# Gated projection in twelve-bit parts: its weights fetched, summed and split at fixed places ahead, every engine there kept in the written order

## The chip, the cores and the metric

The kernel runs on one core of a Trainium2 chip. The metric is device time in microseconds (us) of one execution. A core has a TensorE (PE in the profile, with its weight loads as PEld), a VectorE (DVE), a ScalarE (ACT), a GpSimd (POOL), and SyncE (SP), which here issues nearly all DMA transfers. Each engine works through its own list of instructions in order and waits on semaphores for the others.

## The reference, cut to what matters

A graph network: layer norm and ReLU of x, a batch norm, one graph convolution, four layers of cross attention and a gated feed-forward part, a second graph convolution, and two residuals. The changed code computes the two lines with `geglu_w` below.

```python
N, D, BS, M, DC, H, DH, L, E = (1024, 512, 16, 256, 512, 8, 64, 4, 16384)
h = _gcn(h, src, dst, gcn_in_w, gcn_in_b, n)
for i in range(L):
    a = _attn(_ln(h, ln2_w[i], ln2_b[i]), cond, Wq[i], Wk[i], Wv[i], Wo[i])
    h = h + a
    u = _ln(h, ln3_w[i], ln3_b[i]) @ geglu_w[i] + geglu_b[i]      # 1024x512 @ 512x4096
    val, gate = jnp.split(u, 2, axis=-1)
    f = val * jax.nn.gelu(gate, approximate=False)                # 1024x2048
    h = h + f @ ffo_w[i] + ffo_b[i]                               # 1024x2048 @ 2048x512
h = _gcn(h, src, dst, gcn_out_w, gcn_out_b, n)
```

## The kernel before, in words

**Seven products for eight.** All the large matrix products use Strassen-Winograd's form: a 2x2 block product by seven block products (numbered 0 to 6) and sums of blocks before and after them. In the gated projection the two column halves of the left operand are the value half and the gate half of the weights, so one pass gives value and gate of both halves of the rows.

**The stage.** The feed-forward part of a layer goes in four column blocks r = 0 to 3 of 512 values, each in four chunks c = 0 to 3 of 128. Block r = 0 is computed in plain fp32 (`Quad`, `geglu`). Blocks r = 1 to 3, that is twelve chunks in each of four layers, 48 in all, are objects of the class `Chunk`, in which each fp32 operand of six of the seven products is split into two parts of twelve bits and multiplied in the faster fp32r format: high times high and low times low (`begin`, line 1143), the result scaled on ACT (`scale`, L1151) or on DVE (`scale_onto`, L1155), and then the product of the sums added (`end`, L1160). Product 2 stays in plain fp32 (L1195).

**What a chunk needs.** Its weights are loaded by four DMAs on SP (L1125) into a tall tile `gxa` of 128x1024 and a low tile `gxb` of 128x512. POOL makes four block sums in place (L1127 to L1130). Then `split_left` makes three parts of each tile: the high part on ACT (L1101), the low part on DVE (L1102), and their sum on POOL (L1103). The tall parts feed products 0, 5, 6 and 4, the low ones 1 and 3. The split right operands are made once for a layer (`begin_right`, `finish_right`).

**What a chunk does.** `steps` is a generator: products 0, 5, 6, 4, 1, 3 begin in that order, their ends follow as the scalings come back, DVE adds the running sums s1, u2, u3 (L1184, L1186), makes the gate's input g1 (L1190), ACT applies Gelu (L1168), product 2 is added to the bank of product 4 (L1195), and DVE forms the two outputs (L1199, L1201, L1207) in `fT`. The loop over (r, c) interleaves the steps of a chunk with the last steps of the chunk before it. `sums_of_f` (L1275 to L1279, all on DVE) then makes the block sums that the output projection needs. After chunk 0 of the next block r stands the output projection of the block r - 1, `ffn_out`, in two halves of rows; its sums are added into `hall` and `kept` (L1306, L1310, L1318). `out_weights` makes the block sums of its weights on POOL (L216 to L219).

**What sets the order.** The program is written as a dataflow. A planner with its own model of durations places each instruction on its engine: of the instructions that it holds ready it takes the one written first, so work written later can go ahead of work that is not ready. The order written by hand holds only where `tc.keep_in_program_order` is put around an instruction; in this stage those are the matmuls of the chunks and of the `ffn_out` calls inside the loop. Wide tiles come from a pool of 36 `slot`s (128x1024 fp32), narrow ones from a pool of 10 `t512` tiles (128x512); a tile's first writer waits until the tile that had its room has been read for the last time. There are eight PSUM banks.

**How far ahead.** Two chunks are built before the loop and one more in each turn, after the chunk's fourth step, so that a chunk's transfer, sums and splits are written two chunks ahead of its use, and are placed by the planner.

Of the kernel before, what the change touches and what calls it, by code (L numbers as in the profile page):

```python
# [17 lines left out]
P = 128  # L18
# [7 lines left out]
def gnn_kernel(  # L26
# [1071 lines left out]

    def split_left(x, h, l, s):

        nc.scalar.mul(h.bitcast(F32R), x, INWARD * TINY)  # L1101
        nc.vector.scalar_tensor_tensor(l.bitcast(F32R), h, -1.0 / TINY, x, OP.mult, OP.add)  # L1102
        nc.gpsimd.tensor_tensor(s.bitcast(F32R), h, l, OP.subtract)  # L1103

    class Chunk:


        def __init__(self, l, r, c):
            self.n, self.c = f"{l}_{r}_{c}", c
            self.cv = l * 2 * DFF // P + r * KC + c  # L1110
            tall = [slot(f"g{n}a_{self.n}") for n in "xhls"]
            low = [t512(f"g{n}b_{self.n}") for n in "xhls"]
            self.last = t512(f"g4_{self.n}")[:, :2 * P].rearrange("p (k c) -> p k c", k=2)
            tall, low = ([t.rearrange("p a b -> p (a b)") for t in tall], low)

            def blocks(t):
                return t.rearrange("p (b k c) -> p b k c", k=2, c=P)

            self.parts = [[blocks(t) for t in of] for of in (tall, low)]
            a, b = (of.pop(0) for of in self.parts)  # L1120
            for k, (to, n) in enumerate(((a, 2), (b, 1))):
                for j in range(2):
                    c0 = j * DFF + r * D + c * P
                    of = geglu_w[l][2 * k * P:2 * (k + 1) * P, c0:c0 + P]
                    nc.sync.dma_start(to[:, n * j], of.rearrange("(k p) f -> p k f", p=P))  # L1125
            t = nc.gpsimd
            t.tensor_tensor(a[:, 3], a[:, 2], b[:, 1], OP.add)  # L1127
            t.tensor_tensor(a[:, 2], a[:, 0], a[:, 2], OP.subtract)
            t.tensor_tensor(a[:, 1], a[:, 3], a[:, 0], OP.subtract)
            t.tensor_tensor(self.last, b[:, 0], a[:, 1], OP.subtract)  # L1130
            for of in tall, low:
                split_left(*of)
# [4 lines left out]

        def begin(self, i):

            to = self.banks[i] = bank(f"g{i}_{self.n}")  # L1140
            for which in range(2):
                for k in range(2):
                    tc.keep_in_program_order(nc.tensor.matmul(  # L1143
                        to, self.part(i, which).bitcast(F32R)[:, k, :],
                        self.rights[i][which].bitcast(F32R)[:, k, :],
                        start=which + k == 0, stop=which + k == 2, skip_group_check=True))
            return to

        def scale(self, i):
            to = self.begin(i)  # L1150
            nc.scalar.mul(to, to, 1.0 + TINY)  # L1151

        def scale_onto(self, i, term):
            to = self.begin(i)
            nc.vector.scalar_tensor_tensor(to, to, 1.0 + TINY, term, OP.mult, OP.add)  # L1155

        def end(self, i):
            to = self.banks[i]
            for k in range(2):
                tc.keep_in_program_order(nc.tensor.matmul(  # L1160
                    to, self.part(i, 2).bitcast(F32R)[:, k, :],
                    self.rights[i][2].bitcast(F32R)[:, k, :],
                    start=False, stop=k == 1, skip_group_check=True))
            return to

        def gate(self, to, of):
            cg = self.cv + DFF // P
            nc.scalar.activation(to, of, AF.Gelu, bias=gcols[:, cg:cg + 1])  # L1168

        def steps(self):  # L1170
# [3 lines left out]
            add = nc.vector.tensor_tensor  # L1174
            self.banks = {}
            self.scale(0)
            yield
# [8 lines left out]
            add(u3, self.end(6), u2, OP.add)  # L1186
# [3 lines left out]
            add(g1, d, u3, OP.add)  # L1190
            self.gate(g1, g1)
            self.scale_onto(3, u3)
            yield
            for k in range(2):
                tc.keep_in_program_order(nc.tensor.matmul(  # L1195
                    d, self.last[:, k, :], self.rights[2][:, k, :], start=False, stop=k == 1,
                    skip_group_check=True))
            v1 = acc_tile(f"gv1_{n}")
            nc.vector.scalar_tensor_tensor(v1, d, bias, u2, OP.add, OP.add)  # L1199
            f0, f1 = (self.fT[i][self.c // 2][:, self.c % 2, :] for i in range(2))  # L1200
            add(f1, v1, g1, OP.mult)  # L1201
            yield
# [4 lines left out]
            nc.vector.scalar_tensor_tensor(f0, a, bias, g0, OP.add, OP.mult)  # L1207
# [62 lines left out]
    def sums_of_f(fT, s, c):  # L1270
# [3 lines left out]
        if c < 2:  # L1274
            nc.vector.tensor_tensor(a21, a11, a21, OP.subtract)  # L1275
        else:
            nc.vector.tensor_tensor(s2, a22, a21, OP.subtract)
            nc.vector.tensor_tensor(s1, s2, a11, OP.add)
            sums_of_f.last = nc.vector.tensor_tensor(s4, a12, s2, OP.subtract)  # L1279
# [10 lines left out]
    def ffn_out(l, r, s, left, right, kept, each=lambda ins: ins):  # L1290
# [14 lines left out]
        def add(to, of):  # L1305
            nc.vector.tensor_tensor(to, halves_of(of), to, OP.add)  # L1306

        product(0, a, True)
        if r:
            nc.vector.tensor_tensor(u, a, u, OP.add)  # L1310
# [7 lines left out]
        nc.vector.tensor_tensor(u, b, u, OP.add)  # L1318
# [195 lines left out]
    for l in range(L):  # L1514
# [430 lines left out]
```

## Time and profile before

| | |
|---|---|
| median of 3 runs | 2507.64 us (2507.08 to 2513.2) |
| the profiled execution, its own time | 2509.75 us |
| its span, first to last instruction | 2508.0 us |
| PE busy | 2417.6 us, 96% of the span |
| DVE busy | 1702.0 us, 68% |
| POOL busy | 1031.7 us, 41% |
| ACT busy | 842.4 us, 34% |
| mean granted clock of TensorE | 0.990 |

An instruction row names the line, the engine, the operation, what it writes and reads, the shapes, the count, the busy time and the mean of one, and the idle time of the engine just before with what ended it. A row of waits says who waited, for whom, for how long in total, how often, and the longest. In a timeline the bracket behind a row is the engine's idle time before it. A row of the windows view gives, for a stretch of the span, each engine's busy time and, in the column PEclk, the clock that TensorE was granted (1.00 is full speed). Busy times of PE are of a pipeline: a matmul's bar is longer than the distance to the next.

### The profile page before, as it was taken

Reading aid. Unit: us, or ns where it says so; the run is one execution under the profiler, and the core shown is the slowest. Engines: PE = TensorE matmul, PEld = TensorE weight load, DVE = VectorE, ACT = ScalarE, POOL = GpSimd, SP = SyncE. Lnnn points to the kernel's source line nnn. Section 1 sums busy time; section 2 is a strip of 40 time slices with the busy share of each in tenths; the row PEclk is TensorE's granted clock in tenths of the full one; section 3 lists DMA queues with packets and bytes.
Section 4 is the critical chain, followed back from the end, with each engine's and each line's share of the span. In section 5 each row is a group of like instructions: output and inputs, shape, how many; then the busy total and the mean of one; then the engine's idle time right before and its main releaser. Section 6 shows DMA issues by size and latency. Waiting matters only on the chain. (4 is left out here: it accounts for less than half of the span.)

```text
span 2508.0 us, 35114 instructions
## 1 busy us (share of the span) xinstructions
PE 2417.6 (96%) x13032; PEld 1888.5 (75%) x13032; DVE 1702.0 (68%) x3248; ACT 842.4 (34%) x1784; POOL 1031.7 (41%) x1059
## 2 busy tenths in 40 slices
PE   8999999999999999989999999999999999999999
PEld 5778886667787887567787888467777888567687
DVE  9656567777676557876776556777685556786764
ACT  7323334333213334342313333433223333433320
POOL 0433444265553223275453224264464322445541
PEclk9999999999999999999999999999999999999999
DMA  5422220111312210111221221011131031011140
GB/s 176 131 75 95 97 85 18 42 51 35 121 34 78 96 64 18 39 37 42 68 97 68 77 77 34 7 53 50 43 131 68 14 122 51 1 51 42 42 143 35
DMA packets 118066, 163.56 MB, mean 65 GB/s; under 512 B 9256, under 2 KB 66928, under 8 KB 117888
## 3 DMA queue, kind: packets, MB, share of 16 engines
q1 hardware_dynamic: 115792, 155.81, 19.1%
q0 software_dynamic: 1376, 4.30, 0.5%
q8 instruction: 107, 1.75, 0.3%
q10 hardware_dynamic: 720, 1.11, 0.1%
q14 instruction: 71, 0.58, 0.1%
HBM read 138.12 MB, written 23.07 MB: 64 GB/s over the span
## 5 line engine op out<-in xcount | busy, mean ns | idle before, releaser
L1151 ACT ACTIVATE g<-g 128x512 f32<-128x512 f32 x192 | 110.7, 579 | 349.4 <-PE g L1143 349.4
L1103 POOL TENSOR_TENSOR gsa<-gha,gla 128x1024 fp32r<-128x1024 f32 x48 | 131.8, 2746 | 193.1 <-DVE gla L1102 193.1
L1160 PE MATMUL g<-gr,gsa 128*128 128x512 f32 x384 | 128.2, 416 | 40.2 <-ACT g L1151 40.2
L1127 POOL TENSOR_TENSOR gxa<-gxa,gxb 128x256 f32<-128x256 f32 x48 | 41.1, 856 | 294.4 <-DMA gxa<-in_L_gnn_geglu_w_dram 250.8
L799 ACT ACTIVATE pr<-sc,nmax 128x256 f32<-128x256 f32 x256 | 118.4, 473 | 91.6 <-DVE nmax L794 91.1
L1143 PE MATMUL g<-gr,gha 128*128 128x512 f32 x384 | 144.3, 458 | 0.0
L300 PE MATMUL fa<-wff,fT 128*128 128x256 f32 x512 | 122.7, 383 | 5.0 <-DVE kept L1310 5.0
L1143 PE MATMUL g<-gl,gla 128*128 128x512 f32 x384 | 124.2, 406 | 0.0
L300 PE MATMUL pa_v<-wv,ct 128*128 128x256 f32 x512 | 124.0, 385 | 0.0
L997 POOL TENSOR_TENSOR kr<-ct,ct 128x256 f32<-128x256 f32 x48 | 36.8, 767 | 211.8 <-DVE pr L804 207.1
L1160 PEld LDWEIGHTS g<-gr,gsa 128*128 128x128 f32 x384 | 75.0, 199 | 61.8 <-issue 36.3
L300 PE MATMUL pc_v<-wv,ct 128*128 128x256 f32 x512 | 121.0, 379 | 0.0
L300 PE MATMUL pd_v<-wvs,ct 128*128 128x256 f32 x512 | 120.9, 379 | 0.0
L300 PEld LDWEIGHTS fa<-wff,fT 128*128 128x128 f32 x512 | 97.5, 192 | 25.7 <-DVE kept L1310 8.2
L300 PEld LDWEIGHTS pa_v<-wv,ct 128*128 128x128 f32 x512 | 94.9, 190 | 22.5 <-issue 9.2
L794 DVE TENSOR_REDUCE nmax<-sc 128x2 f32<-128x512 f32 x128 | 83.7, 679 | 41.2 <-PE sc L787 41.2
L1102 DVE SCALAR_TENSOR_TENSOR gla<-gha,gxa 128x1024 fp32r<-128x1024 f32 x48 | 58.6, 1220 | 73.5 <-ACT gha L1101 73.5
L300 PEld LDWEIGHTS pd_v<-wvs,ct 128*128 128x128 f32 x512 | 97.3, 190 | 13.2
L300 PEld LDWEIGHTS pc_v<-wv,ct 128*128 128x128 f32 x512 | 97.0, 190 | 13.0
L1195 PE MATMUL g<-ln3T,g 128*128 128x512 f32 x192 | 93.1, 607 | 11.3 <-DVE g L1190 11.3
L1168 ACT ACTIVATE g<-g,gcols 128x512 f32<-128x512 f32 x96 | 67.4, 702 | 104.7 <-DVE g L1190 93.6
L1143 PEld LDWEIGHTS g<-gr,gha 128*128 128x128 f32 x384 | 75.8, 197 | 35.0 <-issue 21.0
(518 smaller groups left out, 6366.5 us busy)
## 6 DMA issues: line engine op xcount, KB each, us to landing
ct<-cond_dram SPq DMA_DIRECT2D x72, 512.0 KB, 5.2
wff<-in_L_gnn_ffo_w_dram SPq DMA_DIRECT2D x32, 512.0 KB, 3.8
cond_dram<-ct SPq DMA_DIRECT2D x24, 512.0 KB, 3.0
gxb<-in_L_gnn_geglu_w_dram SPq DMA_DIRECT2D x96, 128.0 KB, 2.2
gxa<-in_L_gnn_geglu_w_dram SPq DMA_DIRECT2D x96, 128.0 KB, 2.3
cond<-in_L_gnn_cond_dram SPq DMA_DIRECT2D x32, 256.0 KB, 4.9
ct<-cond_dram SPq DMA_DIRECT2D x24, 256.0 KB, 5.3
wk<-in_L_gnn_Wk_dram SPq DMA_DIRECT2D x8, 512.0 KB, 3.8
```

The costliest lines, as they stand in the source:

```text
L300: each(nc.tensor.matmul(at, left[:, k, l0:l1], right[:, k, r0:r1], start=start and n == 0 and k == 0, stop=n == len(cols_of) - 1 and k == ...
L794: nc.vector.tensor_reduce(nmax, ps3, AX.X, OP.max, negate=True)
L799: nc.scalar.activation(pr3[:, a, :], ps3[:, a, :], AF.Exp, bias=nmax[:, a:a + 1], accum_out=tot[:, a:a + 1])
L997: t.tensor_tensor(to, of, less, OP.subtract)
L1102: nc.vector.scalar_tensor_tensor(l.bitcast(F32R), h, -1.0 / TINY, x, OP.mult, OP.add)
L1103: nc.gpsimd.tensor_tensor(s.bitcast(F32R), h, l, OP.subtract)
L1127: t.tensor_tensor(a[:, 3], a[:, 2], b[:, 1], OP.add)
L1143: tc.keep_in_program_order(nc.tensor.matmul(to, self.part(i, which).bitcast(F32R)[:, k, :], self.rights[i][which].bitcast(F32R)[:, k, :], ...
L1151: nc.scalar.mul(to, to, 1.0 + TINY)
L1160: tc.keep_in_program_order(nc.tensor.matmul(to, self.part(i, 2).bitcast(F32R)[:, k, :], self.rights[i][2].bitcast(F32R)[:, k, :], start=Fa ...
L1168: nc.scalar.activation(to, of, AF.Gelu, bias=gcols[:, cg:cg + 1])
L1195: tc.keep_in_program_order(nc.tensor.matmul(d, self.last[:, k, :], self.rights[2][:, k, :], start=False, stop=k == 1, skip_group_check=True))
```

## The change

The changed code does the same arithmetic on the same tiles, with these differences.

- All instructions of a chunk on ACT, DVE and POOL, and the adds of the `ffn_out` calls inside the loop, are put in `tc.keep_in_program_order` (short: `pin`), like the matmuls.
- The constructor of `Chunk` only loads. Sums and splits are methods (`sums`, `split`), called at three places (`aside`) within the steps of the running chunk n: the sums of chunk n + 2 before product 4, the split of the low tile of chunk n + 1 before product 1, the split of the tall tile of chunk n + 2 after product 3, and then the load of chunk n + 3.
- The running chunk does products 0 and 5 in its first step (before: 0 alone); the ends of the previous chunk follow, and its last output is one step later.
- Ahead of the loop the loads, sums and splits of the first chunks stand between the two halves of the first `ffn_out` and between the calls of `finish_right`.
- `sums_of_f` for c below 2 goes from DVE to POOL in blocks r = 1 to 3.
- `out_weights` is called at c = 3 of the block (c = 2 of the last block) in place of c = 1.
- The tile for product 2's weights (`last`) is half a `t512` tile shared by two chunks; before each chunk had one. The parts' tiles are taken at the split and not with the load.

```diff
     def split_left(x, h, l, s):
-        nc.scalar.mul(h.bitcast(F32R), x, INWARD * TINY)
-        nc.vector.scalar_tensor_tensor(l.bitcast(F32R), h, -1.0 / TINY, x, OP.mult, OP.add)
-        nc.gpsimd.tensor_tensor(s.bitcast(F32R), h, l, OP.subtract)
+        pin(nc.scalar.mul(h.bitcast(F32R), x, INWARD * TINY))
+        pin(nc.vector.scalar_tensor_tensor(l.bitcast(F32R), h, -1.0 / TINY, x, OP.mult, OP.add))
+        pin(nc.gpsimd.tensor_tensor(s.bitcast(F32R), h, l, OP.subtract))
...
+        def sums(self):
+            a, b = (columns_of(x) for x in self.x)
+            for to, x, y, op in ((a[:, 3], a[:, 2], b[:, 1], OP.add),
+                                 (a[:, 2], a[:, 0], a[:, 2], OP.subtract),
+                                 (a[:, 1], a[:, 3], a[:, 0], OP.subtract),
+                                 (self.last, b[:, 0], a[:, 1], OP.subtract)):
+                pin(nc.gpsimd.tensor_tensor(to, x, y, op))
+
+        def split(self, low):
+            if low:
+                to = [t512(f"g{n}b_{self.n}") for n in "hls"]
+            else:
+                to = [flat(slot(f"g{n}a_{self.n}")) for n in "hls"]
+            split_left(self.x[low], *to)
+            self.parts[low] = [columns_of(t.bitcast(F32R)) for t in to]
...
             self.banks = {}
             self.scale(0)
-            yield
             self.scale(5)
             yield
             s1, u2, u3 = (acc_tile(f"g{x}_{n}") for x in ("s1", "u2", "u3"))
-            nc.scalar.copy(s1, self.end(0))
+            pin(nc.scalar.copy(s1, self.end(0)))
             self.scale(6)
             yield
-            add(u2, self.end(5), s1, OP.add)
+            add(u2, self.end(5), s1)
+            yield
+            aside[0]()
             self.scale(4)
-            add(u3, self.end(6), u2, OP.add)
+            add(u3, self.end(6), u2)
+            aside[1]()
             self.scale_onto(1, s1)
             g1 = acc_tile(f"g1_{n}")
             d = self.end(4)
-            add(g1, d, u3, OP.add)
+            add(g1, d, u3)
             self.gate(g1, g1)
             self.scale_onto(3, u3)
+            aside[2]()
             yield
...
-    def sums_of_f(fT, s, c):
+    def sums_of_f(fT, s, c, t=nc.vector, each=lambda ins: ins):
...
-        Chunk.rights = {i: finish_right(f"gl_{l}_{i}", *begun[i]) for i in SPLIT}
-        Chunk.rights[2] = right[2]
         chunks = [(r, c) for r in range(1, R) for c in range(KC)]
-        ready = [Chunk(l, *chunks.pop(0)), Chunk(l, *chunks.pop(0))]
...
+        load()
+        prepare(0, None)
...
+        finish_rights(0, 5)
+        ffn_out(l, 0, 0, left_of_f(fT, fS), wff, kept)
+        prepare(0, False, True)
+        finish_rights(6, 4)
+        load()
+        prepare(1, None)
+        ffn_out(l, 0, 1, left_of_f(fT, fS), wff, kept)
+        finish_rights(1, 3)
+        prepare(1, False)
+        load()
         raw_out = load_out(l, 1)
-        for s in range(2):
-            ffn_out(l, 0, s, left_of_f(fT, fS), wff, kept)
...
+                def sum_next():
+                    prepare(1, None)
+                def split_low():
+                    prepare(0, True)
+                def split_next():
+                    prepare(1, False)
+                    load()
+                flow = chunk.steps([sum_next, split_low, split_next])
...
-                if chunks:
-                    ready.append(Chunk(l, *chunks.pop(0)))
                 if c == 0:
                     if r > 1:
                         for s in range(2):
-                            ffn_out(l, r - 1, s, left_of_f(fT, fS), wff, kept,
-                                    tc.keep_in_program_order)
+                            ffn_out(l, r - 1, s, left_of_f(fT, fS), wff, kept, pin)
                         raw_out = load_out(l, r)
                     fT, fS = f_slots(l, r)
-                elif c == 1:
+                elif c == (KC - 1 if r + 1 < R else KC - 2):
                     wff = out_weights(nc.gpsimd, l, r, raw_out)
```

`prepare(n, ...)` calls `sums` (for None) or `split` (False: tall, True: low) of the n-th chunk that waits in `ready`.

More of the change, by code (lines that the diff above doesn't have):

```diff
@@ L1110, in __init__ @@
             self.cv = l * 2 * DFF // P + r * KC + c
[L1111 to L1121, printed above, removed]
+            self.x = [flat(slot(f"gxa_{self.n}")), t512(f"gxb_{self.n}")]
+            if c % 2 == 0:
+                Chunk.room = t512(f"gy_{self.n}")
+            self.last = columns_of(Chunk.room)[:, c % 2]
+            for k, n in enumerate((2, 1)):
                 for j in range(2):
@@ L1136, in part, with multiply @@
             return self.parts[n // 4][which][:, n % 4]
+        def multiply(self, i, which, to, start, stop):
+            for k in range(2):
+                pin(nc.tensor.matmul(to, self.part(i, which)[:, k, :],
+                                     self.rights[i][which].bitcast(F32R)[:, k, :],
+                                     start=start and k == 0, stop=stop and k == 1,
+                                     skip_group_check=True))
         def begin(self, i):
             to = self.banks[i] = bank(f"g{i}_{self.n}")
[L1141 to L1146, printed above, removed]
+            self.multiply(i, 0, to, True, False)
+            self.multiply(i, 1, to, False, True)
             return to
```

90 lines of the change are left out of this document (51 added, 39 removed).

## The prediction

> **What bounds the kernel now.** I read the page first, then PE's own waits, then the timelines around the longest of them, then the clock. The page:
>
> ```profile
> span 2508.0 us, 35114 instructions
> PE 2417.6 (96%) x13032; PEld 1888.5 (75%) x13032; DVE 1702.0 (68%) x3248; ACT 842.4 (34%) x1784; POOL 1031.7 (41%) x1059
> ```
>
> PE is the bound, with 90 us of idle time in the span. The change adds and removes no matmul, so it can win back only idle time of PE and slow time of PE. The rows of waits on PE that lie in the changed stage:
>
> ```profile
> PE g L1160 <- ACT g L1151: 40.2, 12, 4.2
> PE g L1195 <- DVE g L1190: 11.3, 20, 1.3
> PE fa L300 <- DVE kept L1310: 5.0, 8, 0.7
> PE fd L300 <- DVE fs L1278: 4.2, 3, 1.4
> ```
>
> One wait carries nearly half of the 90 us: the last products of a chunk (L1160) wait for the scaling on ACT (L1151), 12 times, three in each layer. In the first layer they are one of 1.78 us at the stage's first chunk and two of 4.13 us later (8 x 4.13 + 4 x 1.78 = 40.2). The timelines of PE, ACT and POOL around one of 4.13 us:
>
> ```profile
> 522.01 0.62 PE L1160 MATMUL g<-gr,gsb 128*128 128x512 f32 x2
> 526.76 0.70 PE L1160 MATMUL g<-gr,gsa 128*128 128x512 f32 x2 [4.13 <-ACT g L1151]
> ...
> 528.07 1.06 PE L1143 MATMUL g<-gl,gla 128*128 128x512 f32 x2
> 528.92 1.06 PE L1160 MATMUL g<-gr,gsb 128*128 128x512 f32 x2
> ...
> 515.30 0.58 ACT L1151 ACTIVATE g<-g 128x512 f32<-128x512 f32 x1 [0.67 <-PE g L1143]
> 523.95 1.06 ACT L1101 ACTIVATE gha<-gxa 128x1024 fp32r<-128x1024 f32 x1 [8.06 <-POOL gxa L1129]
> ...
> 526.04 1.05 ACT L1151 ACTIVATE g<-g 128x512 f32<-128x512 f32 x2
> ...
> 516.16 1.30 POOL L216 TENSOR_TENSOR wffs<-wff 128x512 f32<-128x512 f32 x1
> ...
> 520.46 1.28 POOL L219 TENSOR_TENSOR wffs<-wff,wffs 128x512 f32<-128x512 f32 x1
> 521.69 0.74 POOL L1127 TENSOR_TENSOR gxa<-gxa,gxb 128x256 f32<-128x256 f32 x1
> ```
>
> The reader is to see one queue behind another. POOL did the four sums of `out_weights` first (516.16 to 521.7), then the block sums of a later chunk. ACT had that chunk's split (L1101) at the head of its line and sat 8.06 us before it; the scalings (L1151), whose products were long there, stood behind it. PE had nothing else in its written order.
>
> The stall costs more than its length. After it a pair of matmuls starts 0.85 us after the last (528.07 to 528.92). At full speed the distance is 0.46 us, below. The windows view of all eleven stretches of the gated stages with half the clock (first and last row, and the sum), and of a plain chunk, of the next, and of the one with the stall:
>
> ```profile
> 489.83:493.25 3.42, 3.42 (x10) 2.65 (x9) 2.30 (x5) 1.57 (x3) 3.42 (x3) 0.50 0.00 0
> ...
> 2346.68:2353.51 6.83, 4.68 (x11) 3.74 (x12) 4.58 (x4) 4.34 (x8) 5.21 (x4) 0.50 0.27 77
> sum 51.21, PE 46.23 PEld 36.36 DVE 36.51 ACT 24.67 POOL 47.75; mean PE 4.20 PEld 3.31 DVE 3.32 ACT 2.24 POOL 4.34
> ...
> 499.98:510.09 10.11, 10.11 (x42) 7.44 (x41) 9.07 (x11) 4.92 (x9) 7.80 (x6) 1.00 0.19 52
> 510.09:520.68 10.59, 10.26 (x42) 7.45 (x41) 9.36 (x11) 4.22 (x8) 8.80 (x6) 1.00 0.18 50
> 520.68:538.05 17.37, 12.11 (x42) 8.52 (x41) 10.82 (x13) 7.61 (x12) 12.41 (x11) 0.90 0.11 31
> 501.31 0.62 PE L1160 MATMUL g<-gr,gsb 128*128 128x512 f32 x2
> 501.77 0.62 PE L1160 MATMUL g<-gr,gsa 128*128 128x512 f32 x2
> ```
>
> PE is busy 46.23 us at clock 0.50; at full speed the same work is 46.23 x 0.46 / 0.85 = 25.0 us, so 21.2 us are lost to the clock. A chunk is 10.11 us on PE without stalls, and in that time DVE works 9.07 us and POOL 7.80: both are close behind PE.
>
> A rule to weigh here: the Trainium skill, "TensorE: Matmul & The Clock Gate", section "Why this matters for your kernels", asks for no idle gap over some 3 us, since a longer one puts the clock back to half. This trace is stricter: the stretch from 489.83 follows a stall of only 1.78 us, and three of the four stalls of that size were followed by one. By the page those three would cost nothing beside themselves; by the trace they do.
>
> **The change, part by part.** *The weights' work moves ahead.* Counts stay: four DMAs, four POOL sums, and three splits of each tile per chunk. Their places become fixed: in chunk n ACT splits the low tile of n + 1 behind the scaling of product 4, and the tall one of n + 2 behind the gate, with sums that POOL is told to make in the same chunk. The 8.06 us in front of L1101 came of a split placed where its sums were not made. Is POOL in time in the new order? I walk it on PE's clock from the chunk's first matmul, groups of four matmuls 0.92 us, of two 0.46, the four of L1195 1.83, with these rows:
>
> ```profile
> L1127 POOL TENSOR_TENSOR gxa<-gxa,gxb 128x256 f32<-128x256 f32 x48 | 41.1, 856 | 294.4 <-DMA gxa<-in_L_gnn_geglu_w_dram 250.8 <-PE g L1160 42.4 <-DMA gxb<-in_L_gnn_geglu_w_dram 1.1
> L1128 POOL TENSOR_TENSOR gxa<-gxa 128x256 f32<-128x256 f32 x48 | 38.0, 791 | 3.8
> L1129 POOL TENSOR_TENSOR gxa<-gxa 128x256 f32<-128x256 f32 x48 | 43.8, 912 | 0.0
> L1103 POOL TENSOR_TENSOR gsa<-gha,gla 128x1024 fp32r<-128x1024 f32 x48 | 131.8, 2746 | 193.1 <-DVE gla L1102 193.1
> L1103 POOL TENSOR_TENSOR gsb<-ghb,glb 128x512 fp32r<-128x512 f32 x48 | 76.1, 1585 | 0.0
> L217 POOL TENSOR_TENSOR wff<-wff,wff 128x512 f32<-128x512 f32 x16 | 24.5, 1532 | 1.3
> L1275 DVE TENSOR_TENSOR fT<-fT,fT 128x512 f32<-128x512 f32 x32 | 31.6, 988 | 0.0
> L1277 DVE TENSOR_TENSOR fs<-fT,fT 128x512 f32<-128x512 f32 x32 | 35.3, 1102 | 0.4
> L1186 DVE TENSOR_TENSOR gu<-g,gu 128x512 f32<-128x512 f32 x48 | 32.8, 683 | 4.2 <-PE g L1160 4.2
> L1207 DVE SCALAR_TENSOR_TENSOR fT<-g,gcols,g 128x512 f32<-128x512 f32 x48 | 35.5, 739 | 0.0
> L1168 ACT ACTIVATE g<-g,gcols 128x512 f32<-128x512 f32 x96 | 67.4, 702 | 104.7 <-DVE g L1190 93.6 <-PE g L1160 11.1
> L1101 ACT ACTIVATE gha<-gxa 128x1024 fp32r<-128x1024 f32 x48 | 50.4, 1050 | 116.4 <-POOL gxa L1129 116.3
> L1101 ACT ACTIVATE ghb<-gxb 128x512 fp32r<-128x512 f32 x48 | 29.5, 614 | 0.0
> ```
>
> The end of product 5 leaves PE at 6.43, with its drain 6.6. DVE does u2 (0.69) and the last output of n - 1 (0.74): 8.0. POOL then makes the sum of f that the change gives it; its nearest row, L217, says 1.53: 9.6. The three sums that the tall split reads take 0.86 + 0.79 + 0.91 = 2.56: 12.1. ACT's tall split then ends at 13.2, and the scaling of product 0 of chunk n + 1 behind it (0.58) at 13.8. PE wants it for the end of product 0 at 10.11 + 4.13 = 14.24. So the stall of 4.13 us goes, with a margin of 0.4 us: what is late next is POOL. POOL's work per chunk is 3.5 + 2.75 + 1.59 + 1.53 = 9.4 us of 10.11, so it can keep up, but with little room. The cost of a late POOL lies between nothing and 0.4 us (as much again as the margin) in the 24 chunks that carry a sum of f on POOL: 0 to 10 us; I take 2, as the rows used are means that already hold POOL's slow cases.
>
> *The order on DVE.* It now does u2, last output, sums of f, u3, low split, L1155, g1. In a chunk without sums of f on DVE, g1 comes at 6.6 + 0.69 + 0.74 + 4 x 0.68 = 10.75, and the L1195 of the next chunk, now behind two products, starts at 10.11 + 1.84 = 11.95: no wait. In a chunk behind c = 2 or 3 three sums of f (some 1.1, 0.9 and 0.9 us) stand ahead of u3: g1 at 13.6, 1.7 us late. Rows overlap by about 0.08 us, so nine instructions make it 0.9. Half of these chunks go straight into an output projection that covers it, which leaves 12 in the kernel: 11 to 20 us, against the 11.3 us that the same wait costs now. I take +3, ends 0 and +9. Moving L1275 saves DVE 24 x 0.99 us, which only lengthens cover.
>
> *`out_weights` two chunks later.* Its four sums, 5.5 us on POOL (516.16 to 521.7), now run in the last chunk of the block and in the next one's first, where POOL has 2 to 3 us free in each and no sum of f. The output projection reads them after that chunk. I cost it at nothing; without this cover it delays the tall split, and behind it DVE's adds of the projection (the 5.0 us row of L1310), by up to 5.5 us in 8 places, 44 us.
>
> *Slots.* SP issues as many DMAs as before. Right operands (17), `kept` (1), f and its sums (7) and the raw output weights (2) leave 9 slots of 36, 7 while `wffs` exists; three parts each for n and n + 1 and one tile for n + 2 are 7. The tile of n + 3 needs the room that the tall split of n + 2 gives back some 13 us into the chunk, which leaves about 6 us until POOL wants it. The transfer is hidden: four issues at about half a microsecond, and the landing:
>
> ```profile
> gxa<-in_L_gnn_geglu_w_dram SPq DMA_DIRECT2D x96, 128.0 KB, 2.3
> ```
>
> *The first chunk.* The pieces ahead of the loop stand earlier in the text, but ACT must now do the tall split of the second chunk before the first chunk's scalings, and POOL waited before it:
>
> ```profile
> 480.09 2.74 POOL L1103 TENSOR_TENSOR gsa<-gha,gla 128x1024 fp32r<-128x1024 f32 x1 [12.02 <-DVE gla L1102]
> 488.43 0.73 PE L1160 MATMUL g<-gr,gsa 128*128 128x512 f32 x2 [1.78 <-ACT g L1151]
> ```
>
> If DVE still makes that `gla` as late, the second chunk's sums come at 484 to 487 and its split at 488, and the 1.78 us become about 3; if it comes earlier, the stall goes. The four stalls and their three slow stretches (10.25 us, 4.7 lost) cost 11.8 us; the ends are -11.8 and +8. I take half the gain, -5.9.
>
> *The sum,* against the profiled execution's 2509.75 us. Eight stalls: -33.1. Slow stretches behind them: 21.2 - 4.7 = 16.5. First chunks: -5.9. POOL late: +2. g1 late: +3. That is 2459.2. The median of the runs shown stands 2.1 us below the profiled one, so 2457.
>
> **The rivals.**
> - *Slower: ACT's line in written order.* Every chunk now has a split ahead of the next scalings. If POOL's sums are later than the margin by more than about 1.4 us, each such stall reaches the size that halved the clock and costs 1.78 + 1.57 = 3.4 us; in 24 chunks 80 us, 2537. For it: POOL was busy 8.80 of 10.59 us in the chunk from 510.09, and two engines meet there. Against: with that load PE lost only 0.33 us in it. It decides at the 50.6 us of the sum above, 15 such stalls.
> - *The stall moves with `out_weights`.* Half of the eight stalls come back at the turn of the blocks: about +28, 2485. For it: POOL's tight sum; against: the projection's cover.
> - *All of it goes,* the rest of the first chunks' stalls (-5.9), the present g1 waits and what I added to them (-14.3) and POOL's 2: 2435. For it: DVE loses 24 us of work, and L1195 gets 0.92 us of room.
> - *It does not do what it says:* the slots run out, transfers wait as before (250.8 us in the row of L1127), the stalls stay: 2505.
>
> The Trainium skill, "GPSIMD Engine Reference", section "Engine selection", advises VectorE for elementwise work with two inputs, GpSimd being about twice as slow. The rows agree in direction, 1.53 against 0.99 us; by the page's factor the sum of f would take 1.98 us and eat the margin of 0.4, about 1 us in all more than I took.
>
> **How the numbers follow.** The forecast has 0.42; all gone 0.20; the moved stall 0.14; no effect 0.07; slower 0.17. The forecast's own range, from its terms' ends, is 2446 to 2485 (-5.9, -3 and -2; +13.9, +6 and +8). The range 2428 to 2512 leaves out most of the slower case and a little below the best. A measurement here tells about 0.3% (7.5 us) from no change: faster 0.77, same 0.05, slower 0.18.
>
> **What would show it.** Right: no wait of PE on L1151 of 4 us, full clock through the stage, ACT without idle time of 8 us before L1101, `gxa` sums never behind L216 to L219 when ACT needs them. A wait of L1195 on L1190 of 0.9 to 1.7 us once a block would confirm the DVE walk. Wrong: many waits of 1 to 2 us on L1151, one per chunk, with half the clock after them; or waits of the output projection on POOL's `wffs`.

## The result and the profile after

The changed kernel took 2509.26 us (median of 12 runs, 2505.73 to 2510.82), the kernel before 2508.51 us beside it (12 runs, 2505.83 to 2513.2). The ratio is 1.0 with a 95% interval of 0.9991 to 1.0009: no difference that can be measured, where 2457 us had been forecast. The profiled execution took 2509.91 us against 2509.75.

The head of the page of the kernel after:

```profile
span 2508.1 us, 35093 instructions
PE 2418.3 (96%) x13032; PEld 1887.7 (75%) x13032; DVE 1740.1 (69%) x3224; ACT 840.8 (34%) x1784; POOL 1052.3 (42%) x1083
```

DVE has 24 instructions fewer and is busy for 38.1 us more (1702.0 before). The prediction had counted on the reverse, 24 us less ("DVE loses 24 us of work"). PE's waits after (who waited, for whom, us in total, times, the longest):

```profile
PE g L1215 <- DVE g L1190: 37.2, 23, 3.1
PE fa L300 <- DVE kept L1329: 14.2, 8, 3.3
PE fc L300 <- DVE hall L1325: 10.3, 4, 2.6
...
PE fb L300 <- DVE fs L1296: 1.3, 3, 0.5
```

The row that carried the forecast, L1160 on ACT's L1151 with 40.2 us, is gone altogether. In the place of the four rows shown of before (40.2 + 11.3 + 5.0 + 4.2 = 60.7 us) stand 37.2 + 14.2 + 10.3 + 1.3 = 63.0 us, and every one of them waits for DVE. The time at half the clock is the same too. The windows view of the thirteen stretches of the gated stages at half the clock (length, busy times of PE, PEld, DVE, ACT and POOL, then the clock, the DMA share and GB/s; first row and the sum):

```profile
531.90:538.73 6.83, 6.05 (x10) 3.48 (x11) 4.67 (x6) 3.16 (x5) 3.93 (x3) 0.50 0.00 0
...
sum 51.22, PE 48.17 PEld 30.43 DVE 34.47 ACT 21.35 POOL 17.89; mean PE 3.71 PEld 2.34 DVE 2.65 ACT 1.64 POOL 1.38
```

51.22 us against 51.21 before; both are fifteen times 3.41 us, and that the counts are equal is chance. The stalls on ACT and their slow stretches were exchanged for stalls on DVE with slow stretches of the same total length.

Why DVE is late is seen around the first wait of 3.1 us, behind the chunk r = 1, c = 2 (the timelines of DVE, POOL and PE):

```profile
520.94 2.00 DVE L1104 SCALAR_TENSOR_TENSOR gla<-gha,gxa 128x1024 fp32r<-128x1024 f32 x1 [1.41 <-ACT gha L1103]
...
523.63 2.33 DVE L1220 TENSOR_TENSOR fT<-gv,g 128x512 f32<-128x512 f32 x1
...
527.15 0.79 DVE L1296 TENSOR_TENSOR fs<-fT,fT 128x512 f32<-128x512 f32 x1
527.97 1.11 DVE L1297 TENSOR_TENSOR fs<-fs,fT 128x512 f32<-128x512 f32 x1
529.00 1.22 DVE L1298 TENSOR_TENSOR fs<-fT,fs 128x512 f32<-128x512 f32 x1
530.15 0.68 DVE L1190 TENSOR_TENSOR gu<-g,gu 128x512 f32<-128x512 f32 x1
...
531.95 0.68 DVE L1190 TENSOR_TENSOR g<-g,gu 128x512 f32<-128x512 f32 x1
...
520.59 1.27 POOL L1105 TENSOR_TENSOR gsb<-ghb,glb 128x512 fp32r<-128x512 f32 x1
523.02 2.40 POOL L1105 TENSOR_TENSOR gsa<-gha,gla 128x1024 fp32r<-128x1024 f32 x1 [1.16 <-DVE gla L1104]
...
526.65 1.88 POOL L1139 TENSOR_TENSOR gxa<-gxa 128x256 f32<-128x256 f32 x2
528.61 1.06 POOL L1139 TENSOR_TENSOR gy<-gxb,gxa 128x256 f32<-128x256 f32 x1
...
532.68 2.07 PE L1215 MATMUL g<-ln3T,gy 128*128 128x512 f32 x2 [3.10 <-DVE g L1190]
```

DVE has no gap between 520.94 and the end of g1 at 532.6; PE waits 3.10 us for that g1. Within that time the tall split takes 2.00 us where it took 1.22 before, and the sums of f 0.79 to 1.22 where L1190, of the same size, takes 0.68. Look at the ends. `gla` ends at 522.94, 1.08 us after POOL's `gsb` (521.86). L1220 ends at 525.96, 0.54 us after `gsa` (525.42). L1297 ends at 529.08, 0.55 us after the two sums of L1139 (528.53), L1298 at 530.22, 0.55 us after the next (529.67). Each began while POOL's instruction ran, and each ended a fixed time after it. So they were not slowed in proportion: they stood still until POOL had done. It holds for the whole kernel: 39 DVE instructions of 128x1024 with two inputs in SBUF began while a POOL sum ran, and all ended 1.080 to 1.086 us after that sum, while the other 33 took 1.21 to 1.23 us. Of the 152 of 128x512 in the changed stage that began so, 143 ended 0.546 to 0.556 us after it; the other nine began in its last 0.06 us and took their free time. DVE instructions with an input in PSUM, such as L1190 and L1173, take 0.68 us beside POOL as without it. The Trainium skill, "SBUF — State Buffer", section "SBUF: two separate sides", says this: VectorE and GpSimd have a pair of ports in common, held for a whole instruction by the one that starts first, and a VectorE instruction with two SBUF inputs contends for it only with a GpSimd instruction that reads SBUF. The trace agrees, with the 0.55 and 1.08 us above.

The groups of the splits and of POOL's sum of f after, and the low split by duration (least, median and greatest, in ns):

```profile
L1104 DVE SCALAR_TENSOR_TENSOR gla<-gha,gxa 128x1024 fp32r<-128x1024 f32 x48 | 76.5, 1594 | 51.3 <-ACT gha L1103 51.3
L1104 DVE SCALAR_TENSOR_TENSOR glb<-ghb,gxb 128x512 fp32r<-128x512 f32 x48 | 50.4, 1050 | 0.0
L1294 POOL TENSOR_TENSOR fT<-fT,fT 128x512 f32<-128x512 f32 x24 | 30.9, 1288 | 217.1 <-DVE fT L1226 217.1
...
L1104 DVE SCALAR_TENSOR_TENSOR glb<-ghb,gxb x48: 674/1270/1632, 478.2 to 2412.1; 128x512 fp32r<-128x512 f32 x48
```

The line of the low split in the kernel before, in the same view:

```profile
L1102 DVE SCALAR_TENSOR_TENSOR glb<-ghb,gxb x48: 677/684/689, 479.9 to 2406.2; 128x512 fp32r<-128x512 f32 x48
```

Before, both splits ran one behind the other while POOL waited for the first of them, so all 48 of each ran free. Apart, and with POOL's sums between, most of them meet a POOL instruction. Added up over both splits, the sums of f, the output `fT<-gv,g`, the low parts of the right operands and the adds of `kept` into `hall`, DVE stood for 99 us before and 147 us after (the time above that of the free ones). These 48 us less the 24 instructions saved (16 us at 0.68) are most of the 38.1 us.

### The profile page after: what moved, and what is told of

It reads as the page before. It is cut to its first block, busy times and chain, and to the rows that moved or that the text cites. A ratio compares the mean times of both kernels' runs of the same rounds, so it can differ in the third digit from the quotient of the medians.

```text
span 2508.1 us, 35093 instructions
## 1 busy us (share of the span) xinstructions
PE 2418.3 (96%) x13032; PEld 1887.7 (75%) x13032; DVE 1740.1 (69%) x3224; ACT 840.8 (34%) x1784; POOL 1052.3 (42%) x1083
## 5 line engine op out<-in xcount | busy, mean ns | idle before, releaser
L1105 POOL TENSOR_TENSOR gsa<-gha,gla 128x1024 fp32r<-128x1024 f32 x48 | 115.9, 2415 | 175.3 <-DVE gla L1104 170.5
L300 PE MATMUL fa<-wff,fT 128*128 128x256 f32 x512 | 125.6, 386 | 14.2 <-DVE kept L1329 14.2
L1215 PE MATMUL g<-ln3T,gy 128*128 128x512 f32 x192 | 103.3, 665 | 37.2 <-DVE g L1190 37.2
L1155 PE MATMUL g<-gr,gsa 128*128 128x512 f32 x384 | 121.4, 398 | 0.9
L1155 PE MATMUL g<-gr,gha 128*128 128x512 f32 x384 | 122.0, 399 | 0.0
L1294 POOL TENSOR_TENSOR fT<-fT,fT 128x512 f32<-128x512 f32 x24 | 30.9, 1288 | 217.1 <-DVE fT L1226 217.1
L1155 PE MATMUL g<-gl,gla 128*128 128x512 f32 x384 | 119.0, 391 | 0.0
L1104 DVE SCALAR_TENSOR_TENSOR gla<-gha,gxa 128x1024 fp32r<-128x1024 f32 x48 | 76.5, 1594 | 51.3 <-ACT gha L1103 51.3
L1215 PEld LDWEIGHTS g<-ln3T,gy 128*128 128x128 f32 x192 | 37.4, 205 | 75.3 <-DVE g L1190 46.9
L804 DVE TENSOR_SCALAR pr<-pr,inv 128x256 f32<-128x256 f32 x256 | 90.4, 395 | 2.9
```

Of the source, the lines that this page charges most:

```text
L300: each(nc.tensor.matmul(at, left[:, k, l0:l1], right[:, k, r0:r1], start=start and n == 0 and k == 0, stop=n == len(cols_of) - 1 and k == ...
L804: scores.last = nc.vector.tensor_scalar(pr3[:, a, :], pr3[:, a, :], inv[:, a:a + 1], None, OP.mult)
L1104: pin(nc.vector.scalar_tensor_tensor(l.bitcast(F32R), h, -1.0 / TINY, x, OP.mult, OP.add))
L1105: pin(nc.gpsimd.tensor_tensor(s.bitcast(F32R), h, l, OP.subtract))
L1155: pin(nc.tensor.matmul(to, self.part(i, which)[:, k, :], self.rights[i][which].bitcast(F32R)[:, k, :], start=start and k == 0, stop=stop a ...
L1215: pin(nc.tensor.matmul(d, self.last[:, k, :], self.rights[2][:, k, :], start=False, stop=k == 1, skip_group_check=True))
```

## The experiments

Two theories at the start. A, the order: the sums of f stand ahead of u3 and g1 in DVE's written order, and that makes g1 late. B, the neighbour: DVE's instructions last longer beside POOL's sums, and that makes it late. In some expectations B is worded as stretching, and C is the effect of the pins alone. Times are medians, and ratios, with their 95% intervals, are to the kernel before.

**The sums of f of c = 2 and 3 behind the next chunk's step.**

```diff
-            sums_of_f(fT, fS, c, *((nc.gpsimd, pin) if c < 2 else (nc.vector, pin)))
+            if c < 2:
+                sums_of_f(fT, fS, c, nc.gpsimd, pin)
...
                 next(flow)
+                if before:
+                    late_sums((c - 1) % KC)
```

> The three sums of f on DVE (c = 2 and 3) are written behind the next chunk's whole step, so behind its g1, in place of ahead of u3. Theory A (their place in DVE's written order makes g1 late): the wait of L1215 on g1, 37.2 us with 3.1 at the longest in the changed kernel, falls below 10 us with none over 1 us, the half-clock stretches behind it go, and the time is 2465 to 2480. Theory B (DVE is late because POOL now works beside it and stretches its splits): the longest wait stays at 2 us or more, and the time stays within 8 us of the changed kernel's 2509.

2552.3 us, ratio 1.0176 (1.0159 to 1.0193). The waits:

```profile
PE fd L300 <- DVE fs L1297: 75.1, 11, 8.4
PE g L1215 <- DVE g L1190: 10.6, 20, 0.8
```

g1 was nearly in time again, as A said, but the output projection that stands right behind now waited up to 8.4 us for the sums. Neither theory had expected a slower kernel: both had looked at g1 alone. DVE is full here, and what is put behind is late in its turn.

**Only the sums of c = 2 behind the next step.**

```diff
-            sums_of_f(fT, fS, c, *((nc.gpsimd, pin) if c < 2 else (nc.vector, pin)))
+            if c != 2:
+                sums_of_f(fT, fS, c, *((nc.gpsimd, pin) if c < 2 else (nc.vector, pin)))
...
+                if before and c == 3:
+                    sums_of_f(fT, fS, 2, nc.vector, pin)
```

> Only the sums of f of c = 2 are written behind the next chunk's step; those of c = 3 stand where the changed kernel has them, ahead of the output projection that reads them. Theory A (place): the eight waits of 3.1 us on g1 fall below 1 us and nothing takes their place, 2470 to 2480. Theory B (DVE is full from the last chunk of a block to the output projection, since POOL stretches its work): what L1215 no longer waits, the projection's first bank waits for instead (L1329, 14.2 us now, to 30 us or more), 2490 to 2515.

2514.28 us, 1.0017 (1.0008 to 1.0027).

```profile
PE fa L300 <- DVE kept L1329: 30.9, 8, 3.9
PE fd L300 <- DVE fs L1297: 11.0, 11, 2.6
...
PE g L1215 <- DVE g L1190: 10.2, 20, 0.8
```

The 27.0 us that g1 gained stand in the two rows above it (+16.7 and +11.0). Here the order decided which product waits, not how much is waited for.

**Pins on matmuls alone.**

```diff
-    pin = tc.keep_in_program_order
+    def pin(ins):
+        if ins.ins.engine == mybir.EngineType.PE:
+            tc.keep_in_program_order(ins)
+        return ins
```

> All new places stay, but the order on ACT, DVE and POOL is left to the planner again; only matmuls are pinned. Theory A: the planner puts u3 ahead of some sums of f, the wait on g1 falls below 20 us, and the time is 2480 to 2500. Theory B: no effect of the order, 2505 to 2512. Theory C (what helped was the pins, the places do nothing): the waits of 4 us on ACT's scaling come back, 2505 or more.

2515.93 us, 1.0029 (1.0017 to 1.004).

```profile
PE g L1158 <- ACT g L1172: 69.5, 20, 7.7
PE g L1218 <- DVE g L1193: 11.0, 8, 1.4
```

With the planner free, ACT's scalings stand behind its splits again, worse than before, and g1 is late in 8 places only. At the first of the long waits POOL does `out_weights` (532.59 to 539.03 us), at its new place, once more ahead of a chunk's sums, and ACT sits 8.10 us before that chunk's split. So inside the changed kernel the pins are needed to be rid of the wait on ACT, and the longer waits on DVE come with them.

**All sums of f on POOL.**

```diff
-            sums_of_f(fT, fS, c, *((nc.gpsimd, pin) if c < 2 else (nc.vector, pin)))
+            sums_of_f(fT, fS, c, nc.gpsimd, pin)
```

> All sums of f go to POOL, at the same place in the text. Theory A: DVE's line is free of them, the wait on g1 falls below 12 us as in the run before; POOL has some 4 us more in two chunks of four, so the output projection may wait for it; 2470 to 2495. Theory B: POOL does more beside DVE, the splits get longer (above 1.6 and 1.05 us in the mean), and the time is 2505 or more.

2541.6 us, 1.014 (1.0123 to 1.0157).

```profile
PE fa L300 <- DVE kept L1329: 29.1, 8, 3.8
PE fd L300 <- POOL fs L1297: 23.4, 11, 2.5
...
L1104 DVE SCALAR_TENSOR_TENSOR gla<-gha,gxa 128x1024 fp32r<-128x1024 f32 x48 | 87.3, 1819 | 115.9 <-ACT gha L1103 115.9
```

Most of what A expected to gain went again. DVE has 72 instructions fewer, which had taken 87 us, but is busy only 45.9 us less (1694.2): with more sums on POOL the tall split took 1819 ns in the mean. The wait on g1 fell to 15.4 us, but the output projection waited for POOL as well.

**The sums of c = 0 and 1 back on DVE.**

```diff
-            sums_of_f(fT, fS, c, *((nc.gpsimd, pin) if c < 2 else (nc.vector, pin)))
+            sums_of_f(fT, fS, c, nc.vector, pin)
```

> The sums of f of c = 0 and 1 go back to DVE (this part of the change alone is undone). Theory A: g1 comes 0.7 us or more later in 24 more chunks, 2518 to 2535. Theory B: DVE gets 24 instructions of 0.68 us more, POOL loses 24 of 1.29 us which it did beside DVE, and these chunks have room on DVE; 2500 to 2515.

2497.56 us, 0.9951 (0.9934 to 0.9967).

```profile
PE 2410.7 (97%) x13032; PEld 1887.0 (76%) x13032; DVE 1730.7 (69%) x3248; ACT 838.7 (34%) x1784; POOL 1025.3 (41%) x1059
...
L1104 DVE SCALAR_TENSOR_TENSOR gla<-gha,gxa 128x1024 fp32r<-128x1024 f32 x48 | 62.7, 1307 | 47.0 <-ACT gha L1103 47.0
```

DVE does 24 instructions more and is busy 9.4 us less than in the changed kernel; the splits run nearly free (1307 and 786 ns). In the changed kernel 20 of the 48 low splits had stood behind this very sum on POOL (L1294). The run is faster than either theory had it: this part of the change costs about half a per cent by itself.

**Three of POOL's four block sums replaced by transfers, then by memsets.**

```diff
+                    if k == 0:
+                        nc.sync.dma_start(columns_of(self.x[k])[:, n * j + 1],
+                                          of.rearrange("(k p) f -> p k f", p=P))
...
-            for to, x, y, op in ((a[:, 3], a[:, 2], b[:, 1], OP.add),
-                                 (a[:, 2], a[:, 0], a[:, 2], OP.subtract),
-                                 (a[:, 1], a[:, 3], a[:, 0], OP.subtract),
-                                 (self.last, b[:, 0], a[:, 1], OP.subtract)):
+            for to, x, y, op in ((self.last, b[:, 0], a[:, 1], OP.subtract),):
```

> Three of POOL's four block sums of a chunk's weights are left out; two more transfers fill their blocks with plain weights, so the outputs are not the reference's. POOL has some 2.7 us less per chunk. Theory A: the wait on g1 stays above 25 us and the time within 12 us of 2509. Theory B: the splits on DVE fall back towards 1.22 and 0.68 us, the wait on g1 falls below 15 us, and the time below 2490.

2466.83 us, 0.9838 (0.9822 to 0.9855). Waits, and DVE around the chunk that was shown of after:

```profile
PE fa L300 <- DVE kept L1329: 19.0, 8, 2.4
PE g L1215 <- DVE g L1190: 13.5, 11, 1.3
...
518.88 1.23 DVE L1104 SCALAR_TENSOR_TENSOR gla<-gha,gxa 128x1024 fp32r<-128x1024 f32 x1 [1.13 <-ACT gha L1103]
...
524.33 0.68 DVE L1296 TENSOR_TENSOR fs<-fT,fT 128x512 f32<-128x512 f32 x1
```

The order is that of the changed kernel, but in this chunk the tall split and the sums of f run free, and PE waits 1.20 us in this place instead of 3.10. From the start of the tall split to the end of g1 DVE needs 9.85 us instead of 11.69. So of the 3.10 us 1.2 belong to the order (A), and 1.9 to the standing (B). The first was about what the prediction's walk had given. The half-clock stretches shrink to some 7 us. Over the whole kernel only the tall split is free (1223 ns); the low one, which the expectation had free too, still takes 1091 ns in the mean, since POOL's other sums remain.

Seven memsets of a block put before the one sum that is left:

```diff
+            for k in range(7):
+                pin(nc.gpsimd.memset(a[:, 2 * (k % 2) + 1], 0.0))
             for to, x, y, op in ((self.last, b[:, 0], a[:, 1], OP.subtract),):
```

> As the run with two more transfers in place of three of POOL's sums (2467 us, outputs not the reference's: three of four block sums left out), with seven memsets on POOL at their place, which keep POOL busy but read nothing. Theory B, in the form that DVE's instructions with two inputs in SBUF share their second read with POOL's reads: 2462 to 2475, and the splits keep their lengths. Its rival, that it is POOL's occupied time that holds up the chain: 2485 or more if the memsets take 2 us or more per chunk.

2476.13 us, 0.9867 (0.985 to 0.9883). The memsets, and the tall split beside them:

```profile
L1139 POOL MEMSET gxa<- 128x256 f32 x336 | 88.0, 314 | 0.0
...
L1104 DVE SCALAR_TENSOR_TENSOR gla<-gha,gxa 128x1024 fp32r<-128x1024 f32 x48 | 63.7, 1328 | 45.2 <-ACT gha L1103 45.2
```

88 us of work that reads nothing cost 9.3 us. The 14 DVE instructions of two SBUF inputs and 128x512 that began while a memset ran took 0.67 to 0.69 us, as free. The tall splits lost 0.1 us each in the mean because the memsets had moved POOL's sum of the low parts (`gsb`) into the way of 26 of them. The time lies between the two theories' ranges, and the memsets took 1.83 us per chunk, less than the 2 us that the rival asked for; so a small share for POOL's occupied time is not excluded. But what stands beside memsets runs free: it is POOL's reading instructions that hold DVE.

**The low split right behind the tall one, at the chunk's end.**

```diff
                 def split_low():
-                    prepare(0, True)
+                    pass
...
                     prepare(1, False)
+                    prepare(0, True)
```

> The changed kernel with the low split moved behind the tall one, as a pair at the end of the chunk, as the kernel before pairs them. If sharing with POOL is the cause, both splits fall back to about 1.22 and 0.69 us, one instruction less stands ahead of g1, and the wait on g1 falls from 37 to 20 us or less: 2475 to 2498. If ACT's line is what matters, its scalings come 0.6 us later and PE waits for L1169: 2508 or more.

2499.33 us, 0.9951 (0.9929 to 0.9973).

```profile
PE fa L300 <- DVE kept L1329: 23.9, 8, 3.6
PE g L1215 <- DVE g L1190: 19.4, 11, 2.1
...
L1104 DVE SCALAR_TENSOR_TENSOR gla<-gha,gxa 128x1024 fp32r<-128x1024 f32 x48 | 58.7, 1222 | 69.6 <-ACT gha L1103 62.5 <-DMA gxa<-in_L_gnn_geglu_w_dram 7.0
```

Paired, the tall split runs free again and the low one nearly so (1222 and 729 ns), though POOL does as much as in the changed kernel. The place of a DVE instruction against POOL's decides whether it stands. Other instructions took over a part of it: the last sum of f (L1298) went from 1098 to 1285 ns in the mean, and the projection's wait on L1329 from 14.2 to 23.9 us.

**All right operands finished ahead.**

```diff
-        finish_rights(0, 5)
+        finish_rights(0, 5, 6, 4, 1, 3)
```

> The changed kernel with all six finish_right ahead of the first projection half, as the kernel before has them. The wait of the first projection on L1325 (4 x 2.57 us, with a half-clock stretch behind three) comes of two finish_right of 3.4 and 2.3 us on DVE beside POOL's sums: if so it goes, finish_right falls from 1.57 and 2.08 to 1.4 us, and 2492 to 2502. If the first chunk then waits for its splits on ACT as before, nothing is won: 2504 to 2512.

2506.46 us, 0.9985 (0.9975 to 0.9995).

```profile
PE g L1155 <- ACT g L1169: 9.5, 4, 2.4
```

The low parts of the right operands run free (1.21 us) and the 10.3 us at the first projection go, but a wait on ACT at the first chunk of a layer takes their place with 9.5. The wait on g1 stays at 36.7 us.

**`out_weights` alone: in the kernel before at the new place, at c = 2, and in the changed kernel at the old place.**

```diff
-                elif c == 1:
+                elif c == (KC - 1 if r + 1 < R else KC - 2):
                     wff = out_weights(nc.gpsimd, l, r, raw_out)
```

> The kernel before, with out_weights called at c = 3 (c = 2 of the last block) and nothing else of the change. If the eight stalls of 4.13 us came of out_weights ahead of a chunk's sums alone, they go, with their half-clock stretches: 49.6 us less, 2455 to 2475. If POOL's sums in the last chunk and the next block's first only move the stall, or stretch DVE's sums of f there, 2485 to 2515.

2480.63 us, 0.9876 (0.9855 to 0.9898). This one line, with nothing else of the change, is faster than both kernels. Four of its waits, and POOL at the chunk that had stalled:

```profile
PE fc L300 <- DVE hall L1306: 15.2, 12, 1.7
PE g L1195 <- DVE g L1190: 14.0, 14, 1.6
PE fc L300 <- POOL wff L217: 7.8, 8, 1.0
PE g L1160 <- ACT g L1151: 7.1, 4, 1.8
...
513.91 1.75 POOL L1103 TENSOR_TENSOR gsb<-ghb,glb 128x512 fp32r<-128x512 f32 x1
515.62 0.74 POOL L1127 TENSOR_TENSOR gxa<-gxa,gxb 128x256 f32<-128x256 f32 x1
```

The block sums follow the split's sum at once, with no `out_weights` between. The eight stalls of 4.13 us are gone (40.2 - 33.1 = 7.1), the half-clock stretches of the gated stages fall from 51.2 to 20.5 us, and both splits stay at 1223 and 684 ns. Of the 49.6 us that the expectation had hoped for some 30 came. The rest went largely to the output projection, which now waits 15.2 us for DVE's adds (L1306, 1.8 us before) and 7.8 us for `out_weights` itself, and into slow stretches that stay.

The kernel before, with `out_weights` at c = 2 in every block:

```diff
-                elif c == 1:
+                elif c == 2:
```

> The kernel before with out_weights at c = 2 in every block. The run with c = 3 (2481 us) still loses 1.0 us to POOL's L217 and 1.67 us behind it at each of eight projections. If POOL has room one chunk earlier, these go and no stall of 4 us comes back: 2460 to 2478. If out_weights gets ahead of a chunk's sums there as at c = 1, the 4 us on ACT's scaling come back: 2495 to 2515.

2480.3 us, 0.988 (0.9864 to 0.9897).

```profile
PE g L1195 <- DVE g L1190: 28.1, 14, 3.1
```

The same time by another split of it: no wait at the projection on POOL, but g1 late by up to 3.1 us.

The changed kernel, with `out_weights` at the old place:

```diff
-                elif c == (KC - 1 if r + 1 < R else KC - 2):
+                elif c == 1:
```

> The changed kernel with out_weights back at c = 1 (this part alone undone). If DVE's stretch beside POOL at the turn of the blocks is the cause, POOL's 5.5 us less there shorten the sums of f and the waits of 3.1 us on g1 to 2.5 or less, while the chunks behind c = 1 take some of it back: 2490 to 2508. If it is the place of the sums in the written order alone, the 3.1 us stay: 2506 to 2515.

2512.56 us, 1.0018 (1.0008 to 1.0027).

```profile
PE g L1155 <- ACT g L1169: 31.2, 8, 3.9
PE g L1215 <- DVE g L1190: 20.3, 23, 1.6
```

The eight stalls on ACT come back, 3.9 us each, with all pins in place. So it was the place of `out_weights` that removed them, in both kernels; in the changed one it does so only under the pins. The g1 waits fall from 3.1 to 1.6 us at the longest, but that does not tell what made them: in the chunk shown of after, POOL does `out_weights` from 538.05 to 544.11 us, behind the wait of 3.10 us. In this run PE has just stalled 3.89 us on ACT in that chunk and then runs at half the clock (523.68 to 530.50 us), so it comes late itself, and its wait on g1 there is 0.42 us.

## Why the prediction was right and wrong

- *Eight stalls gone, -33.1: right,* in size and in cause. It was POOL's `out_weights` ahead of a chunk's sums, shown from both sides by the runs that move it in either kernel.
- *Slow stretches behind them, -16.5: nothing.* 51.21 us became 51.22. The step took the new waits to be too short for the clock, but of the eight of 3.1 us seven were followed by half the clock.
- *First chunks, -5.9: +3.2 in waits.* The four stalls on ACT (7.1 us) went, but the right operands' low parts, now spread between the projection's halves, stood behind POOL's splits, and four waits of 2.57 us on L1325 (10.3 us) came at the first projection. The working had not looked at `finish_right` at all.
- *POOL late, +2: not seen.* No wait of PE on ACT's scalings is left in the list of its waits. The walk's margin of 0.4 us was enough, and the rival by ACT's line, to which it led, fell with it. The price of the sum of f on POOL, 1.53 us by the nearest row, measured 1.29. The 1.98 us that the prediction had from the factor of two in the Trainium skill ("GPSIMD Engine Reference", section "Engine selection") was further off, but not by that factor: it doubled 0.99 us, a mean in which DVE's standing was contained. Against the free 0.68 us the 1.29 are 1.9 times, and the trace agrees with the skill.
- *g1 late, +3: the term that failed.* It measured +25.9 (11.3 to 37.2). The walk had u3 and g1 late by 0.9 to 1.7 us in twelve places; with three of POOL's sums away it is 1.2 us in eleven, so the order was read rightly. What came was eight waits of 3.1 us, of which 1.9 were DVE standing behind POOL, and fifteen shorter ones, 12.4 us in all. The step took its durations from rows of before, where the splits never met POOL's sums, and moved them to places where they do. That is the step that failed.
- *"Moving L1275 saves DVE 24 x 0.99 us": wrong in sign.* Back on DVE, those sums make it 9.4 us less busy than in the changed kernel, and the kernel 0.5% faster than before.
- *`out_weights` at nothing: wrong by some 7 us.* By itself the new place is the gain, 1.2%. But its named risk, a late tall split and behind it DVE's adds of the projection, did come: PE waits 14.2 us for L1329 against 5.0, and 6.8 us with the old place in the changed kernel (the row is not shown). The longest of these waits, with what stands ahead of it on POOL and ACT:

```profile
616.27 1.60 POOL L219 TENSOR_TENSOR wffs<-wff,wffs 128x512 f32<-128x512 f32 x1
...
620.54 1.06 ACT L1103 ACTIVATE gha<-gxa 128x1024 fp32r<-128x1024 f32 x1 [0.16 <-POOL gxa L1139]
...
624.27 3.56 PE L300 MATMUL fa<-wff,fT 128*128 128x256 f32 x8 [3.33 <-DVE kept L1329]
```

The chunk's sums come behind `out_weights`, ACT's tall split behind them, DVE's at 621.63, and L1329 behind that at 623.54. The cover that the prediction counted on was too short here. The rival in which the stall moves with `out_weights` was right so far, with some 7 us (14.2 - 6.8) and not 28.

- *Slots, no effect:* POOL waits 53.3 us for the weights' transfer (L1139 on `gxb`) against the 250.8 us of before, so transfers did not wait as before. The time of that rival, 2505, was near by luck: its mechanism was not what happened.

What the prediction missed in the profiled execution, 50.7 us, lies in four terms: g1 (22.9), the slow stretches (16.5), the projection's wait on L1329 (9.2) and the first chunks (9.1). Against them stand the 2 us for a late POOL and the row of L1278 (4.2 us), which went.

DVE's standing could have been read in the trace of before. There `fT<-gv,g` (L1201) already took 2.11 us between instructions of the same size at 0.7:

```profile
502.10 2.11 DVE L1201 TENSOR_TENSOR fT<-gv,g 128x512 f32<-128x512 f32 x1
```

It ended 0.55 us after POOL's `gsa`. The prediction's own rows, too, have L1275 at 988 and L1277 at 1102 ns, beside 683 for L1186: the standing was in the numbers that were carried over as plain durations.

Open is what the parts would give together: the moved `out_weights` of the kernel before with some of the pins, or the changed kernel with both the paired splits and the sums of f on DVE. That wasn't tried. How much of the fifteen shorter waits on g1 is order and how much standing was not separated either.

## What to carry to other kernels

A duration belongs to its place: before a step of one engine is moved, compare the least and the greatest time of its rows, and see what the engine that can hold it up (here POOL) does at the old place and at the new one. Where one wait carries the forecast, look for the single line that makes it and try that line alone; here it was worth 1.2%, and the rest of the change took it back. An engine that has no gap over a whole chunk got little time back by reordering here: the two runs that moved its sums of f only chose another product to wait, and what helped (0.5% each) was to take its instructions and POOL's sums out of each other's way.

## What the runs showed of the hardware

- A DVE instruction with two inputs in SBUF that begins while POOL reads SBUF ends 0.55 us (128x512) or 1.08 us (128x1024) after POOL's instruction, or after its free 0.68 or 1.22 us where that is later: a low part of a right operand (L1096) that takes 1.21 us free took up to 3.37. One that has begun keeps its time, and POOL's next waits: `gsb` of the kernel before took 1.74 us when it began beside a running DVE instruction of this kind, 1.28 free (medians). With an input in PSUM, or beside a memset, nothing is lost.
- Half the clock followed seven of eight gaps of 3.1 us of PE, three of four of 2.57 us, and two of five between 1.70 and 1.94 us (after, in the gated stages). The Trainium skill's rule of some 3 us that the prediction weighed ("TensorE: Matmul & The Clock Gate", section "Why this matters for your kernels") would have let the last two groups pass; here the trace decides.
- These stretches all begin a whole number of 3.413 us apart, in after as in the other traces. What counted was how much of a gap of PE fell within one such step: with 2.03 us or more each of them was followed by half the clock, in all fourteen traces between 470 and 2440 us, with less than 1.38 us none, and between the two some were. The one gap of 3.1 us without it was cut by the steps' border, with 1.94 us on the longer side.
